# Two exponentials moved ahead of four copies on ScalarE, and the running maxima read from SBUF: one change to a convolution and attention kernel

## The chip, the cores and the metric

The kernel runs on one core of a Trainium2 chip. The core has a matrix engine (TensorE, PE in the profile; PEld is its loading of weights), a vector engine (VectorE, DVE), a scalar engine for activation functions (ScalarE, ACT), GpSimd (POOL) and SyncE (SP), on whose queue this kernel's transfers are issued. Each executes its own instructions in the order of the program and waits on semaphores for the others. Tiles lie in SBUF (128 partitions); results of matrix products lie in PSUM, which has 8 banks of 128x512 fp32 words here, and are taken out by DVE or ACT. The metric is the time of one execution on the device, in microseconds (us); less is better. Unless something else is said, durations come from one profiled execution.

## What is computed

The input x has the shape (8, 512, 32, 32) in fp32. Two layers run, each on a group-normalised x and each added back to it.

```python
# layer 0; cbs(x, w) = silu(batch_norm(conv(x, w)))
t = cbs(gn(x), cv1_w)                       # 1x1, 512 -> 512
ys = [t[:, :256], t[:, 256:]]
for i in range(2):
    yi = ys[-1]
    z = cbs(yi, m_cv1_w[i])                 # 3x3, 256 -> 256
    qkv = conv(z, qkv_w[i])                 # 1x1, 256 -> 768, four heads of 64
    logits = einsum('bhdi,bhdj->bhij', q, k + r) * 64 ** -0.5    # 1024 x 1024
    a = softmax(logits, axis=-1)
    z = einsum('bhij,bhdj->bhdi', a, v)
    ys.append(yi + cbs(z, m_cv2_w[i]))      # 1x1, 256 -> 256
x = x + cbs(concatenate(ys, axis=1), cv2_w) # 1x1, 1024 -> 512
# layer 1: a 1x1 convolution, 512 -> 512, its weights masked and permuted by a gate
x = x + conv(gn(x), w_eff)
```

## The kernel before

**Units.** The attention is cut into 64 units: an image, one of its two bottlenecks, a pair of heads (hp) and a half (512) of the 1024 queries. Sixteen slots of four units follow each other, with the images taken in pairs. A unit holds its logits transposed: the 1024 keys are 8 tiles (KT = 8) of 128 partitions, and one tile is a pair of 128x512 halves, one for each head, stored as one 128x1024 tile `st` in SBUF (the pool `stp` has 10 of them).

**Steps.** A unit is worked off in four steps of two tiles (`for t in range(0, KT, 2)`, lines 1055 to 1082). While unit u is exponentiated and multiplied by its values, the logits of the next unit (`nxt`) are made. In a step:

- `u.soften(t)`, `u.soften(t + 1)` (line 545, DVE): adds to `st` the negated maximum of each query, which lies spread over all partitions in PSUM (`mb`).
- `exponent` (line 549, ACT): the exponential of a 128x1024 tile in place; POOL then adds it in four pieces to the running sum (line 556).
- `lag.values` (line 563, PE): the products of the exponentials with the values, into the one bank `po`. They lag by one step: step 0 works off the last two tiles of the unit before, step 2 tiles 0 and 1 of this unit.
- At step 0 also `before.finish()` (line 577 on PE, the sum's reduction over partitions; line 580 on ACT, the copy of these denominators to `rb`) and `before.divide` (DVE: two reciprocals of 128x256, line 584, and two multiplications of `po` into `q`, line 586). The second of these is the last reader of `po`, so the next unit's first values wait for it.
- `nxt.logits(t)`, `nxt.logits(t + 1)`: eight products on PE in the profile (line 511) fill four PSUM banks; ACT copies each half to `st` (line 518), and from the second tile of a unit on DVE takes the maximum of what was so far (`mx`; of tile 0's `st` at first) and the logits in PSUM, half by half (line 523).
- Last `advance(...)`: convolutions are put onto PE until their share of the slot is reached. A hand-made clock with due times decides which: the 1x1 convolutions cv1, cv2, m_cv2 and that of layer 1 (all line 175 on PE, outputs `cv`, `m` and `l`), the 3x3 convolution by Winograd products (line 313, output `m`), and the projection to q, k and v (lines 175 and 405). ACT takes most of them out of PSUM with a SiLU (line 130, outputs `y`, `m2s`, `cv2s`, `z`) and normalises x (line 165, `x`); DVE adds residuals (line 430 `ybuf` and `res`, line 457 `xr`, line 487 `x2r`).

After the last step, `top` (line 531 on PE, 532 on DVE) transposes and reduces `mx` to one maximum for each query, and `spread` (line 540, `mb`) spreads it.

**What sets the order.** ACT's copies and exponentials are tied in the order in which the program issues them (`act_turn`); DVE's additions of line 545, maxima and a few others by `in_turn`, PE's attention products by `pe_turn`. All other instructions are placed by a scheduler between these, each on its engine, before the kernel runs; their order is fixed then.

**Buffers.** Of PSUM's 8 banks, `mb` holds two, `po` one; the other five (`bank`, line 68) go round among the logits, the denominators, the transposed maxima and all convolutions. A product into such a bank waits until the last reader of what was in it is done. An exponential and a SiLU need different tables on ACT; a switch is an instruction of its own (ACT_TABLE_LOAD), which the profile puts down to the line of the activation after it (130 or 549).

Of the kernel before, what the change touches and what calls it, by code (L numbers as in the profile page):

```python
# [17 lines left out]
ALU = mybir.AluOpType  # L18
# [21 lines left out]
def conv_preact_kernel(ctx: ExitStack, tc: tile.TileContext, x, cv1, cv2, mcv1, qkv, mcv2, bn, rw, rh, conv, s_in, t_in, out):  # L40
    nc = tc.nc
# [23 lines left out]
    def pair(p, tag, name):  # L65
        return p.tile([P, 2, HALF], F32, tag=tag, name=name)

    def bank(name):
        return ps_f.tile([P, HALF], F32, tag="bank", name=name)
# [4 lines left out]
    def flat(t):  # L74
        return t.rearrange("p a b -> p (a b)")
# [106 lines left out]
    def in_turn(instruction):  # L182

        if turn:
            tc.add_manual_dep(instruction.ins, turn.pop().ins.name, IN_ORDER, reason="order of VectorE")
        turn.append(instruction)

    def act_turn(instruction):

        if act_last:  # L190
            tc.add_manual_dep(instruction.ins, act_last.pop().ins.name, IN_ORDER, reason="order of ScalarE")
        act_last.append(instruction)
# [3 lines left out]
    def pe_turn(instruction):  # L196

        if pe_last:
            tc.add_manual_dep(instruction.ins, pe_last.pop().ins.name, IN_ORDER, reason="order of TensorE")
        pe_last.append(instruction)  # L200
# [293 lines left out]
    class Unit:  # L494
# [8 lines left out]
        def logits(self, t):  # L503

            if t == 0:
                self.begin()
            lg = [bank(f"lg_{self.name}_{t}_{h}") for h in range(2)]
            for h in range(2):
                r = slice(HD * h, HD * h + HD)
                pe_turn(  # L510
                    nc.tensor.matmul(  # L511
                        lg[h], self.k[r, ts(t, P)], self.q[r, self.hp, ts(self.half, HALF)], start=True, stop=True
                    )
                )
            st = pair(stp, "st", f"st_{self.name}_{t}")
            self.st.append(st)
            for h in range(2):
                act_turn(nc.scalar.copy(st[:, h], lg[h]))  # L518
            if t == 1:
                self.mx = pair(one, "mx", f"mx_{self.name}")  # L520
            for h in range(2 if t else 0):
                so_far = self.st[0] if t == 1 else self.mx
                in_turn(nc.vector.tensor_tensor(self.mx[:, h], so_far[:, h], lg[h], ALU.max))  # L523

        def top(self):

# [382 lines left out]
    def slot_filler(s):  # L909

        prev = slots[s - 1] if s else (None, 0)
        nxt = slots[s + 1] if s + 1 < len(slots) else (None, 0)
        todo, needed = [], 0.0

        def add(us, g):
            nonlocal needed
            todo.append((us, g))
            needed += us

        im, i = nxt  # L920
        add(8.0, bg.take(8.0))
        if im and i == 1:
            add(7.0, im.conv_m2(0))
            add(0.0, call(im.transform, 1, 3.0, 1.0))
            add(9.0, bg.take(9.0))
        products = im.conv3(i) if im else iter(())
        if prev[1] == 1:
            if im:
                add(21.3, (us for _, us in zip(range(16), products)))
            add(7.0, prev[0].conv_m2(1))  # L930
            add(0.0, call(lambda: finishing(prev[0])))
        if im:
            add(10.7 if prev[1] == 1 else 32.0, products)
            add(7.0, bg.take(7.0))
        if im:
            add(21.0, im.project(i))
        if s + 2 < len(slots) and slots[s + 2][1] == 0:
            add(0.0, call(slots[s + 2][0].load_y))
            add(0.0, call(slots[s + 2][0].transform, 0, 8.0, 1.3))
        rest = SHARE - needed if im else 70.0  # L940
        if rest > 0:
            todo.append((rest, bg.take(rest, wait=True)))
        total = sum(c for c, _ in todo)
        return needed, total, todo
# [77 lines left out]
    for s in range(len(slots)):  # L1022
        needed, total, todo = slot_filler(s)
        state = {"done": 0.0}

        def filler():
            for us, g in todo:
                start = state["done"]
                for cost in g:
                    clock.tick(cost)  # L1030
                    state["done"] += cost
                    yield

                state["done"] = max(state["done"], start + us)

        fill = filler()

        def advance(share):
            goal = max(share * total, min(1.0, share / 0.74) * needed + 0.1)
            while state["done"] < goal:  # L1040
                if next(fill, "end") == "end":
                    break

        steps = 4 * (KT + 2)
        for j in range(4):
            u = units[4 * s + j]
            nxt = units[4 * s + j + 1] if 4 * s + j + 1 < len(units) else None
            base = j * (KT + 2)

            advance((base + 0.7) / steps)  # L1050
            u.top()
            clock.tick(0.9)
            advance((base + 1.4) / steps)
            u.spread()
            clock.tick(0.9)
            advance((base + 2) / steps)
            for t in range(0, KT, 2):
                if before and t == 0:
                    before.finish()
                    clock.tick(0.9)  # L1060
                u.soften(t)
                u.soften(t + 1)
                if t:
                    u.exponent(t)

                lag = u if t else before
                if lag:
                    lag.values((t - 2) % KT)
                    lag.values((t - 1) % KT)
                    clock.tick(2.0)  # L1070
                if before and t == 0:
                    before.divide(0)
                    before.divide(1)
                if nxt:
                    nxt.logits(t)
                    nxt.logits(t + 1)
                    clock.tick(2.0)

                if not t:
                    u.exponent(t)  # L1080
                u.exponent(t + 1)
                advance((base + 4 + t) / steps)
            before = u
        for _ in fill:
            pass
# [62 lines left out]
```

## Time and profile before

| | us |
|---|---|
| median of three runs | 3184.22 (3184.0 to 3186.14) |
| the profiled execution | 3188.51 |
| its span, from the first to the last instruction | 3186.8 |
| mean granted TensorE clock | 0.993 |
| one step, typically | about 9.2 |
| eight products of a step's logits (line 511) | 1.99 |
| eight products of a step's values (line 563) | 1.94 |
| copy of 128x512 from PSUM, ACT (line 518) | 0.596 |
| exponential of 128x1024, ACT (line 549) | 1.068 |
| table load, ACT | 1.283 |
| SiLU of 128x512, ACT (line 130) | 0.777 |
| copy of denominators, ACT (line 580) | 0.583 |
| maximum of 128x512, DVE (line 523) | 0.681 |
| addition of 128x1024, DVE (line 545) | 1.213 |
| reciprocal of 128x256, DVE (line 584) | 1.723 |

A line of the profile's groups names the line of the kernel, the engine, the operation, its output and inputs (names without buffer numbers), the shape and the count; behind the first bar stand the busy time in us and the mean of one in ns, behind the second the engine's idle time just before these instructions and what ended most of it. A timeline's line gives the start and the length in us of a run of like instructions, and in brackets the idle time before it and what ended that. The end of a matrix product is modelled, so products that follow each other overlap by up to 0.1 us in such lines.

A second view of the same execution, in 40 slices, shows that PE is busy throughout:

```profile
PE   7999999999999999999999999999999999999999
DVE  5446576667666676667666676667766676666742
ACT  3255765854655555544656455554656455555631
```

Each digit is the busy share of a slice in tenths; the first slices are the preparation of weights and the first two images, and the units run from about 215 us to 3060 us.

### The profile page before, as it was taken

The page shows a single profiled execution, that of the slowest core. Times are in us where ns is not written, and L with a number is a line of the kernel's source. Part 1 is how long each engine was busy: PE and PEld are TensorE (multiplying, and loading weights), DVE is VectorE, ACT ScalarE, POOL GpSimd, SP SyncE. Part 2 cuts the span into 40 slices and gives each one's busy share as a digit, 9 for nine tenths or more (in the row PEclk, how much of TensorE's full clock was granted, in tenths as well). Part 3 has the DMA queues.
Part 4 walks back from the last instruction along what each step waited for, and adds up shares of the span by engine and source line. Part 5 has one row for each costly group of instructions (what it writes and reads, how often), then busy time and mean ns, then how long its engine had stood idle before and what let it go on. Part 6 is the DMA issues. An engine that isn't in the chain of part 4 may idle for free.

```text
span 3186.8 us, 34171 instructions
## 1 busy us (share of the span) xinstructions
PE 3085.9 (97%) x11668; PEld 1522.9 (48%) x11668; DVE 2050.6 (64%) x2718; ACT 1717.3 (54%) x2347; POOL 1395.3 (44%) x1867
## 2 busy tenths in 40 slices
PE   7999999999999999999999999999999999999999
PEld 3645444454445454454445454454445454453333
DVE  5446576667666676667666676667766676666742
ACT  3255765854655555544656455554656455555631
POOL 2114444446444454445444454355434454455420
PEclk9999999999999999999999999999999999999999
DMA  8851442421233232424233332424233332413366
GB/s 294 287 187 63 154 161 83 149 79 65 88 109 129 93 119 70 148 86 137 89 109 129 119 114 75 139 83 142 90 113 132 110 122 71 145 63 129 110 212 216
DMA packets 142014, 399.35 MB, mean 125 GB/s; under 512 B 13072, under 2 KB 14352, under 8 KB 141840
## 3 DMA queue, kind: packets, MB, share of 16 engines
q1 hardware_dynamic: 141120, 396.94, 36.4%
q8 instruction: 92, 1.51, 0.2%
q14 instruction: 82, 0.67, 0.1%
q10 hardware_dynamic: 720, 0.23, 0.0%
HBM read 317.42 MB, written 79.69 MB: 125 GB/s over the span
## 4 chain that ended last, share of the span: by engine, by line
PE 70%; DVE 7%; ACT 5%; issue 3%; DMA 2%; POOL 1%; ACTq 0%; DVEq 0%; SPq 0%; POOLq 0%
PE m L313 14%; PE cv L175 12%; PE lg L511 11%; PE po L563 11%; PE qk L175 6%; PE l L175 6%; PE v L405 3%; PE m L175 2%; DVE st L545 2%; PE mb L540 2%; ACT st L518 2%; PE mt L531 2%; PE den L577 2%; DVE mx L523 1%; ACT st L549 1%
## 5 line engine op out<-in xcount | busy, mean ns | idle before, releaser
L556 POOL TENSOR_TENSOR sum<-sum,st 128x256 f32<-128x256 f32 x1536 | 1126.1, 767 | 570.1 <-ACT st L549 565.0
L523 DVE TENSOR_TENSOR mx<-mx,lg 128x512 f32<-128x512 f32 x768 | 477.8, 681 | 412.2 <-ACT st L518 412.2
L549 ACT ACTIVATE st<-st 128x1024 f32<-128x1024 f32 x512 | 539.1, 1068 | 340.2 <-DVE st L545 338.8
L518 ACT COPY st<-lg 128x512 f32<-128x512 f32 x1024 | 524.4, 596 | 351.7 <-PE lg L511 306.6
L545 DVE TENSOR_TENSOR st<-st,mb 128x1024 f32<-128x1024 f32 x512 | 603.7, 1213 | 63.6 <-PE mb L540 63.6
L313 PE MATMUL m<-plane,w_m 128*128 128x256 f32 x2304 | 537.4, 388 | 21.8 <-DVE x2r L487 9.0
L556 POOL TENSOR_TENSOR sum<-st,st 128x256 f32<-128x256 f32 x256 | 188.0, 766 | 789.4 <-ACT st L549 789.3
L563 PE MATMUL po<-st,v 128*64 128x512 f32 x2048 | 500.3, 608 | 21.7 <-ACT st L549 14.7
L511 PE MATMUL lg<-q,k 64*128 64x512 f32 x2048 | 513.7, 619 | 1.6 <-ACT y L130 1.5
L313 PEld LDWEIGHTS m<-plane,w_m 128*128 128x128 f32 x2304 | 433.0, 192 | 149.0 <-issue 44.1
L175 PE MATMUL cv<-y,w_cv 128*128 128x512 f32 x1024 | 465.4, 599 | 10.8 <-DVE mx L523 6.2
L511 PEld LDWEIGHTS lg<-q,k 64*128 64x128 f32 x2048 | 178.6, 187 | 330.1 <-issue 266.4
L175 PEld LDWEIGHTS cv<-y,w_cv 128*128 128x128 f32 x1024 | 185.7, 190 | 251.7 <-issue 227.8
L563 PEld LDWEIGHTS po<-st,v 128*64 128x64 f32 x2048 | 128.9, 137 | 327.5 <-issue 228.9
L175 PE MATMUL l<-x,w_l 128*128 128x512 f32 x512 | 235.8, 603 | 10.3 <-DVE mx L523 10.0
L175 PE MATMUL cv<-x,w_cv 128*128 128x512 f32 x512 | 233.4, 603 | 8.5 <-ACT x L165 2.4
L175 PE MATMUL qk<-z,w_qkv 128*128 128x512 f32 x512 | 234.0, 600 | 1.7 <-DVE mx L523 1.7
L584 DVE RECIPROCAL rb<-rb 128x256 f32<-128x256 f32 x128 | 215.4, 1723 | 30.6 <-ACT rb L580 30.5
L532 DVE TENSOR_REDUCE nm<-mt 128x4 f32<-128x512 f32 x128 | 82.4, 685 | 158.6 <-PE mt L531 158.5
L580 ACT COPY rb<-den 128x512 f32<-128x512 f32 x64 | 37.3, 583 | 226.9 <-PE den L577 226.9
L175 PEld LDWEIGHTS l<-x,w_l 128*128 128x128 f32 x512 | 92.7, 190 | 132.3 <-issue 107.2
L175 PEld LDWEIGHTS cv<-x,w_cv 128*128 128x128 f32 x512 | 94.3, 192 | 126.4 <-issue 107.3
(145 smaller groups left out, 2404.3 us busy)
## 6 DMA issues: line engine op xcount, KB each, us to landing
w_m<-w_m SPq DMA_DIRECT2D x96, 768.0 KB, 4.8
w_cv<-in_cv SPq DMA_DIRECT2D x90, 512.0 KB, 3.5
y<-y SPq DMA_DIRECT2D x64, 512.0 KB, 4.4
x<-in_x SPq DMA_DIRECT2D x56, 512.0 KB, 5.4
y<-y SPq DMA_DIRECT2D x64, 256.0 KB, 3.5
k<-r SPq DMA_DIRECT2D x32, 512.0 KB, 3.6
res<-y SPq DMA_DIRECT2D x32, 512.0 KB, 4.0
xr<-in_x SPq DMA_DIRECT2D x32, 512.0 KB, 4.0
```

The lines of the kernel that those rows point to most:

```text
L175: nc.tensor.matmul(ps, w, moving, start=(n == 0), stop=(n == len(terms) - 1))
L313: nc.tensor.matmul(ps[:, ts(co, 256)].rearrange("p (t x) -> p t x", x=F), w[:, co, c, dx], u[:, 9 * c : 9 * c + 8, dx : dx + F], start=(j ...
L405: nc.tensor.matmul(ps[:, ts(j, P)], z[:, c, ts(4 * j4 + j, P)], w[:, c, 512 + P * hp : 512 + P * hp + P], start=(c == 0), stop=(c == IT - 1),)
L511: nc.tensor.matmul(lg[h], self.k[r, ts(t, P)], self.q[r, self.hp, ts(self.half, HALF)], start=True, stop=True)
L518: act_turn(nc.scalar.copy(st[:, h], lg[h]))
L523: in_turn(nc.vector.tensor_tensor(self.mx[:, h], so_far[:, h], lg[h], ALU.max))
L532: nc.vector.tensor_reduce(self.nm[:, h], mt, AX.X, ALU.max, negate=True)
L545: in_turn(nc.vector.tensor_tensor(st, st, flat(self.mb), ALU.add))
L549: act_turn(nc.scalar.activation(st, st, AF.Exp))
L556: nc.gpsimd.tensor_tensor(flat(self.acc)[:, part], flat(so_far)[:, part], st[:, part], ALU.add)
L563: nc.tensor.matmul(self.po[HD * h : HD * h + HD], self.v[:, t, ts(h, HD)], self.st[t][:, h], start=(t == 0), stop=(t == KT - 1),)
L584: nc.vector.reciprocal(self.rb[:, r], self.rb[:, r])
```

## The change

Two edits. In `logits`, the maximum of a tile becomes one operation on the whole 128x1024 pair, which reads the copy `st` in SBUF where it read the two halves in PSUM. In the step's loop, the exponentials of tiles 0 and 1 are issued ahead of the last values of the unit before, of its division and of the next unit's logits; so far both stood behind these. In the other steps the order stays: the first tile's exponential ahead, the second's behind the logits.

```diff
@@ -518,9 +518,10 @@
                 act_turn(nc.scalar.copy(st[:, h], lg[h]))
             if t == 1:
                 self.mx = pair(one, "mx", f"mx_{self.name}")
-            for h in range(2 if t else 0):
+            if t:
+
                 so_far = self.st[0] if t == 1 else self.mx
-                in_turn(nc.vector.tensor_tensor(self.mx[:, h], so_far[:, h], lg[h], ALU.max))
+                in_turn(nc.vector.tensor_tensor(flat(self.mx), flat(so_far), flat(st), ALU.max))
 
         def top(self):
 
@@ -1060,8 +1061,10 @@
                     clock.tick(0.9)
                 u.soften(t)
                 u.soften(t + 1)
-                if t:
-                    u.exponent(t)
+                u.exponent(t)
+                if not t:
+
+                    u.exponent(1)
 
                 lag = u if t else before
                 if lag:
@@ -1076,9 +1079,8 @@
                     nxt.logits(t + 1)
                     clock.tick(2.0)
 
-                if not t:
-                    u.exponent(t)
-                u.exponent(t + 1)
+                if t:
+                    u.exponent(t + 1)
                 advance((base + 4 + t) / steps)
             before = u
         for _ in fill:
```

`flat` views a pair of halves as one row of 1024. `exponent(1)` also issues tile 1's four sums on POOL, which move with it.

## The prediction

> **What bounds the kernel now.** I read the page first, then the list of what TensorE (PE) waits for between 220 and 3030 us (the 64 units), then timelines around single waits.
>
> ```profile
> span 3186.8 us, 34171 instructions
> PE 3085.9 (97%) x11668; PEld 1522.9 (48%) x11668; DVE 2050.6 (64%) x2718; ACT 1717.3 (54%) x2347; POOL 1395.3 (44%) x1867
> ...
> L523 DVE TENSOR_TENSOR mx<-mx,lg 128x512 f32<-128x512 f32 x768 | 477.8, 681 | 412.2 <-ACT st L518 412.2
> L549 ACT ACTIVATE st<-st 128x1024 f32<-128x1024 f32 x512 | 539.1, 1068 | 340.2 <-DVE st L545 338.8
> L518 ACT COPY st<-lg 128x512 f32<-128x512 f32 x1024 | 524.4, 596 | 351.7 <-PE lg L511 306.6
> L545 DVE TENSOR_TENSOR st<-st,mb 128x1024 f32<-128x1024 f32 x512 | 603.7, 1213 | 63.6 <-PE mb L540 63.6
> ```
>
> PE is busy for all but 3186.8 − 3085.9 = 100.9 us. VectorE (DVE) and ScalarE (ACT) idle for over a third of the span, so removing work from DVE shortens nothing by itself. The change can win only PE's waits, and PE loses only where a new wait reaches it. Whose waits these are:
>
> ```profile
> PE po L563 <- ACT st L549: 14.7, 12, 3.7
> PE l L175 <- DVE mx L523: 10.0, 5, 2.6
> PE m L313 <- DVE x2r L487: 9.0, 3, 3.5
> PE cv L175 <- DVE mx L523: 8.2, 7, 2.0
> ...
> PE po L563 <- DVE mx L523: 6.9, 8, 2.3
> ...
> PE m L313 <- DVE mx L523: 2.1, 5, 1.5
> ...
> PE qk L175 <- DVE mx L523: 1.7, 1, 1.7
> ```
>
> Columns: us in total, times, longest. Convolutions (l, cv, m, qk) wait for a maximum because it is the last reader of the PSUM bank they need: 10.0 + 8.2 + 2.1 + 1.7 = 22.0 us. The value products (po) wait for an exponential or, by their label, a maximum: 14.7 + 6.9 = 21.6 us. So 43.6 us are the most that the change can address. One bank wait, and two waits of po:
>
> ```profile
> 1626.27 2.02 ACT L518 COPY st<-lg 128x512 f32<-128x512 f32 x4
> ...
> 1626.86 2.48 DVE L523 TENSOR_TENSOR mx<-mx,lg 128x512 f32<-128x512 f32 x4 [0.46 <-ACT st L518]
> ...
> 1627.61 3.70 PE L175 MATMUL cv<-y,w_cv 128*128 128x512 f32 x8 [1.47 <-DVE mx L523]
> ```
>
> ```profile
> 1441.07 2.02 PE L563 MATMUL po<-st,v 128*64 128x512 f32 x8 [1.23 <-DVE mx L523]
> ...
> 2917.66 3.68 PE L563 MATMUL po<-st,v 128*64 128x512 f32 x8 [3.72 <-ACT st L549]
> ```
>
> In the first, the copy of the first half ends at 1626.87, its maximum at 1627.54, and PE starts 0.07 later: the bank came free 0.67 us after its copy. In the second, the value products of a unit's first tile stand still until its exponential is done, which stands behind the next unit's four copies on ACT.
>
> **What the skill says.** "VectorE: DVE Perf Modes" (section on the TRN2 errata) gives an fp32 tensor_tensor as (N+151)/0.96 ns: 691 for N=512 and 1224 for N=1024. The trace agrees within 2%: 681 for the maxima (whose one source is in PSUM), 1213 for L545's add of 128x1024. "PSUM — Partial Sum Buffer" (PSUM bank collisions) says that two engines may not be in the same bank and quadrant at once, reads included; hence the maximum cannot overlap the copy of the same bank, and the trace shows maxima idle 412.2 us until a copy ends. "ScalarE: Activation LUTs" (What ACT_TABLE_LOAD costs) gives about 1283 ns for a load at every switch between sets of functions, plus a drain of 1380; the trace has the load at 1283 and the next exponential 0.01 after it, so I use 1.28 without the drain. "TensorE: Matmul & The Clock Gate" (HAM clock gate) says that an idle PE falls to half clock; here the 3.72 us wait above is followed by po taking 3.68 instead of 1.94.
>
> **The maxima.** Out: 896 maxima (768 + 128 of the first form) of 0.68. In: 448 of 128x1024, both operands in SBUF, as L545's shape: 1.22. Busy time falls by 896×0.68 − 448×1.22 = 63 us, but back to back they start 0.60 and 1.13 us apart, so a backlogged step gains only 4×0.60 − 2×1.13 = 0.14. Where DVE keeps pace with the copies (0.48 apart), the first maximum now waits for two copies and the step ends 0.48 − 0.14 = 0.34 later. Neither is on PE's path unless DVE ends late. What reaches PE is the bank, free at the copy's end. Eight waits like the one shown (at 343.5, 440.7, 527.6, 908.2, 1457.9, 1627.6, 2179.0, 2348.8) lose 0.7 each, but at 343.5 the maximum was held up by group-norm statistics and all 2.1 go: 7×0.7 + 2.1 = 7.0. Four smaller (near 667, 1191, 1910, 2628) give 0.22 each: 0.9. Together 7.9. The last layer's waits near 1308, 2027 and 2745, with a second some 14 us later (0.66 and 2.3 to 2.6 each, 9.2 in all), I count as nothing: DVE there runs a chain (residual load of 7.35 us, its additions, L545, exponential, copies, maxima) that ends in m's wait for x2r, the 9.0 us above, which takes back what is gained ahead of it.
>
> **The first exponentials.** Tiles 0 and 1 go ahead of the four copies. Nothing is added but their order. In the unit from 1433.10 us (first mb transpose; times below are from such a start) the first exponential ended at 7.91 and po started at 7.96. The second L545 ends at 3.50 and the copy of the denominators (L580) at 2.70, so the two exponentials can run from 2.7 to 4.7, before the first copy at 4.91. Then po's bank decides: its last reader, the second division (L586), ends at 7.38. Gain 0.53, not 1.23. By the same subtraction: units 7, 27, 43, 59: 4×0.53 = 2.1; 28, 44: 0.8; 23, 39, 55: 0.87 each = 2.6 (0.37, and 0.5 because the copies of tile 2 no longer wait for POOL's sum, 45.0 us of ACT's idle time over 23 times); 11, 12, 19: 0.5 + 0.6 + 1.3 = 2.4; 16, 32, 48: 0.6; unit 60: 3.72 becomes 1.7 (division at 7.59, exponential was at 9.56), and 1.5 of its slow matmuls. Sum 2.1 + 0.8 + 2.6 + 2.4 + 0.6 + 3.5 = 12.0.
>
> **What that puts in the way.** ACT executes in the program's order, and that order shows 40 more table loads (262 for 222): exponentials now stand between SiLUs. Forty loads are 51 us of an engine that idles 46%; only those ahead of a copy matter. The worst is unit 3 (start 349.65):
>
> ```profile
> 354.73 0.76 ACT L130 ACTIVATE y<-cv,bn_b,bn_s 128x512 f32<-128x512 f32 x1
> 355.39 0.57 ACT L580 COPY rb<-den 128x512 f32<-128x512 f32 x1
> 356.39 2.05 ACT L518 COPY st<-lg 128x512 f32<-128x512 f32 x4 [0.43 <-PE lg L511]
> 358.46 1.28 ACT L549 ACT_TABLE_LOAD   x1
> 359.75 2.00 ACT L549 ACTIVATE st<-st 128x1024 f32<-128x1024 f32 x2
> ```
>
> After: x, x (to 5.2), load, exponential 0, load, SiLU, denominators, load, exponential 1, copies. From 5.2: 1.28 + 1.07 + 1.28 + 0.78 + 0.57 + 1.28 + 1.07 = 12.5, so the first copy ends near 13.0; it ended at 7.33. The group of cv matmuls that follows needs its bank at 7.69 and waits 12.97 − 7.69 = 5.3. Unit 4 (396.72) has the same order with a late x in it: copy at 16.4 for 11.6, PE waits 4.85 more. After each, slow matmuls: 2 together, by unit 60's case. Ten units have this order; in the other eight (6, 8, 16, 24, 32, 40, 48, 56) copies come some 1.7 later by the same addition, but PE finds their banks free when it asks: 0 (at worst 1.7 each, 13.6). Units 13, 17, 29, 33, 45, 49 put exponential 2 between two loads ahead of the last m2s SiLU, whose bank m's next product wants at 14.74 and gets near 15.3: 6×0.55 = 3.3. Units 20, 36, 52: the later maxima delay a cv2s chain by 0.3: 0.8 (bounds 0 and 3). On POOL the sums start earlier with exponential 1; SP's loads keep their order but for a few swaps, cost 0. Losses 5.3 + 4.85 + 2 + 3.3 + 0.8 = 16.3.
>
> **Sum.** −7.9 − 12.0 + 16.3 = −3.6. On the profiled execution, 3188.51 (span 3186.8 and 1.7 around it), that is 3184.9; on the median shown, 3184.22, it is 3180.6. I say 3180.5.
>
> **Rivals.**
> (1) Small gain as summed, own range 3174 to 3187: 0.42.
> (2) Larger gain. If the last layer's maxima waits go too (9.2) and the banks at units 3 and 4 turn out free, it is 7.9 + 12.0 + 9.2 − 4.1 = 25 us; with only one of the two 13 to 16. I take 19, between these: 3165. For: 43.6 us of waits name these lines. Against: the divisions end at 7.4 to 7.6, and x2r waits for a DMA. 0.27.
> (3) No change, 3184: every earned wait comes back as another's (divisions, x2r). For: PE at 97%. Against: the bank waits have nothing else behind them. 0.09.
> (4) Slower, by one mechanism: table loads and exponentials ahead of the copies hold PSUM banks, at the eight further units too. It decides from the point where a copy ends after PE asks for its bank. Then 3180.6 + 13.6 = 3194. For: five banks only, and units 3 and 4 show it. Against: at several of the eight the copies already stood behind POOL's sum (up to 3.4 us) and end about where they did. 0.22.
>
> 0.2% is 6.4 us, about what can be told from no change. Under 3177.8: nearly all of (2), 0.26, and a good third of (1), 0.16: 0.42. Over 3190.6: three quarters of (4), 0.17, and 0.05 of the others: 0.22. Between: 0.36. The range runs from just under (2)'s 3165 to just under (4)'s 3194: 3163 to 3193.
>
> **What would show it.** Right: no wait of a convolution for a maximum outside the last layer's places; po's first wait in unit 27 at 0.7; 40 more table loads; waits of cv of about 5 us near 357 and 405. Wrong: no such waits, or x2r's 9.0 us gone (then 2), or waits for copies in the eight units (then 4).

## The result: slower by 1.6%

The changed kernel took 3238.68 us in the median (3228.86 to 3240.2), the kernel before 3184.11 (3183.04 to 3186.14): a ratio of 1.016, with a 95% interval from 1.0142 to 1.0178. The prediction was 3180.5 in a range of 3163 to 3193, so both the sign and the range were wrong.

The page of the kernel after, with the rows that answer to those shown of before (the lines of the file have moved by one: 523 is now 524, 545 is 546, 549 is 550, 556 is 557, 563 is 564, 540 is 541):

```profile
span 3237.7 us, 33432 instructions
PE 3106.1 (96%) x11668; PEld 1535.4 (47%) x11668; DVE 2118.6 (65%) x2270; ACT 1770.7 (55%) x2387; POOL 1612.7 (50%) x1867
...
L557 POOL TENSOR_TENSOR sum<-sum,st 128x256 f32<-128x256 f32 x1536 | 1333.5, 902 | 751.1 <-ACT st L550 750.5
...
L524 DVE TENSOR_TENSOR mx<-mx,st 128x1024 f32<-128x1024 f32 x384 | 535.8, 1395 | 444.9 <-ACT st L518 423.8
...
L546 DVE TENSOR_TENSOR st<-st,mb 128x1024 f32<-128x1024 f32 x512 | 603.9, 1213 | 63.6 <-PE mb L541 60.6
```

Of the 51 us by which the span grew, PE's idle time holds 31: 3237.7 − 3106.1 = 131.6 us where it was 100.9. The other 20 are products that took longer: the same 11668 of them are busy for 3106.1 us instead of 3085.9, at a mean granted clock of 0.988 for 0.993. On its losing side the prediction had put slower products at 2 us.

DVE has 448 instructions fewer and is busy for longer, 2118.6 us for 2050.6. POOL does exactly what it did before, 1867 instructions, and is busy for 1612.7 us instead of 1395.3. The two rows that carry this are the maxima, 1.395 us where I had put 1.22, and POOL's sums, 0.902 for 0.767. The addition of L546, from which the 1.22 was taken, still takes 1.213. Besides the operation itself it differs in one thing: its second operand, `mb`, lies in PSUM, while both operands of the new maximum lie in SBUF.

What PE waits for between 220 and 3080 us in the kernel after (us in total, times, longest):

```profile
PE m L313 <- DVE x2r L487: 14.5, 3, 4.8
PE m L313 <- ACT cv2s L130: 13.6, 3, 4.5
PE l L175 <- ACT st L518: 10.0, 5, 2.4
PE m L313 <- ACT st L518: 9.1, 7, 4.1
PE po L564 <- DVE q L587: 8.9, 10, 1.8
PE po L564 <- ACT st L550: 6.5, 4, 2.7
PE mb L541 <- DVE nm L533: 5.3, 4, 4.3
```

The intended part happened. No convolution waits for a maximum any more (22.0 us before), and po's waits for exponentials fell from 14.7 to 6.5. Others took their place: x2r from 9.0 to 14.5, cv2s from 8.2 to 13.6, mb for nm from 0.7 to 5.3, and the same banks' waits for ACT's copies, 10.0 for l and 9.1 for m.

### The profile page after: what moved, and what is told of

Same layout as the page of the kernel before. It is cut to its first block, busy times and chain, and to the rows that moved or that the text cites. A ratio compares the mean times of both kernels' runs of the same rounds, so it can differ in the third digit from the quotient of the medians.

```text
span 3237.7 us, 33432 instructions
## 1 busy us (share of the span) xinstructions
PE 3106.1 (96%) x11668; PEld 1535.4 (47%) x11668; DVE 2118.6 (65%) x2270; ACT 1770.7 (55%) x2387; POOL 1612.7 (50%) x1867
## 3 DMA queue, kind: packets, MB, share of 16 engines
q8 instruction: 93, 1.52, 0.2%
## 4 chain that ended last, share of the span: by engine, by line
PE 64%; DVE 11%; ACT 4%; issue 3%; DMA 2%; POOL 2%; SPq 0%; DVEq 0%; ACTq 0%; POOLq 0%
PE cv L175 14%; PE m L313 11%; PE lg L511 9%; PE po L564 9%; PE qk L175 6%; PE l L175 6%; PE v L405 3%; DVE st L546 3%; DVE mx L524 2%; POOL sum L557 2%; PE mt L532 2%; PE mb L541 1%; PE den L578 1%; DVE rb L585 1%; ACT st L518 1%
## 5 line engine op out<-in xcount | busy, mean ns | idle before, releaser
L557 POOL TENSOR_TENSOR sum<-sum,st 128x256 f32<-128x256 f32 x1536 | 1333.5, 902 | 751.1 <-ACT st L550 750.5
L524 DVE TENSOR_TENSOR mx<-mx,st 128x1024 f32<-128x1024 f32 x384 | 535.8, 1395 | 444.9 <-ACT st L518 423.8
L546 DVE TENSOR_TENSOR st<-st,mb 128x1024 f32<-128x1024 f32 x512 | 603.9, 1213 | 63.6 <-PE mb L541 60.6
L313 PE MATMUL m<-plane,w_m 128*128 128x256 f32 x2304 | 547.7, 393 | 43.8 <-DVE x2r L487 14.5
```

The costliest lines, as they stand in the source:

```text
L313: nc.tensor.matmul(ps[:, ts(co, 256)].rearrange("p (t x) -> p t x", x=F), w[:, co, c, dx], u[:, 9 * c : 9 * c + 8, dx : dx + F], start=(j ...
L524: in_turn(nc.vector.tensor_tensor(flat(self.mx), flat(so_far), flat(st), ALU.max))
L546: in_turn(nc.vector.tensor_tensor(st, st, flat(self.mb), ALU.add))
L557: nc.gpsimd.tensor_tensor(flat(self.acc)[:, part], flat(so_far)[:, part], st[:, part], ALU.add)
```

## The experiments

Two theories stood against each other. T1: two operands in SBUF put DVE and POOL in each other's way, and DVE's lateness costs most of the time. T2: the exponentials and table loads ahead of copies and SiLUs on ACT, rival (4) of the prediction, cost most of it. All ratios are to runs of the kernel before on the same chip; on these later occasions it took 3188 to 3190 us in the median. The ratios are not quotients of the medians, but lie within 0.0012 of them.

| kernel | median us | ratio to before | 95% interval |
|---|---|---|---|
| maxima alone | 3220.49 | 1.0102 | 1.0083 to 1.0120 |
| exponentials alone | 3201.25 | 1.0038 | 1.0024 to 1.0051 |
| maxima alone, without most sums | 3153.05 | 0.9881 | 0.9863 to 0.9900 |
| before, without most sums | 3150.13 | 0.9875 | 0.9859 to 0.9891 |
| maxima of halves, both from the copies | 3258.63 | 1.0215 | 1.0200 to 1.0231 |
| maxima of halves, one from the copies | 3203.20 | 1.0041 | 1.0027 to 1.0055 |
| exponentials ahead from unit 5 on | 3182.69 | 0.9977 | 0.9967 to 0.9987 |
| exponentials unsplit | 3203.65 | 1.0037 | 1.0024 to 1.0050 |
| both of these | 3187.23 | 0.9997 | 0.9989 to 1.0004 |
| exponentials ahead in 18 chosen units | 3173.85 | 0.9955 | 0.9938 to 0.9972 |

### The change taken apart

Maxima alone, the exponentials as before:

```diff
-            for h in range(2 if t else 0):
+            if t:
                 so_far = self.st[0] if t == 1 else self.mx
-                in_turn(nc.vector.tensor_tensor(self.mx[:, h], so_far[:, h], lg[h], ALU.max))
+                in_turn(nc.vector.tensor_tensor(flat(self.mx), flat(so_far), flat(st), ALU.max))
```

> The maxima alone: one 128x1024 maximum from the copies in SBUF, exponentials as before. In the changed kernel a maximum took 1.40 us on average, not the 1.22 of the prediction: 1.22 where no POOL sum ran beside it, 1.52 where one ran for most of it, and POOL's sums took 0.90 for 0.77. Theory T1 (the two operands in SBUF hinder POOL and are hindered by it; late maxima are most of the loss): 3210 to 3240 us, with maxima near 1.4 us and the waits of m for cv2s and x2r long (13 and 14 us in all). Theory T2 (the exponentials and table loads ahead of the copies and SiLUs on ScalarE are most of the loss): 3175 to 3195, the bank waits gone, and cv2s and x2r waits only a little longer than before.

Exponentials alone, the maxima as before:

```diff
-                if t:
-                    u.exponent(t)
+                u.exponent(t)
+                if not t:
+                    u.exponent(1)
...
-                if not t:
-                    u.exponent(t)
-                u.exponent(t + 1)
+                if t:
+                    u.exponent(t + 1)
```

> The exponentials alone: tiles 0 and 1 ahead, maxima from PSUM as before. T1: 3172 to 3190, since the maxima cost 0.68 as before and ScalarE's order costs only the 12 us of units 3 and 4, against 12 us gained. T2: 3205 to 3235, with units 0, 3 and 4 alone longer by 20 us or more, as in the changed kernel (5.6, 13.3 and 5.8 us).

Both parts lose. The maxima cost 1.0%, about 32 us (31 by the medians), as T1 said. The exponentials cost 0.4%, about 12 us, which lies between the two expectations, though units 0, 3 and 4 lose the 20 us of T2 (table below). Their sum, 1.4%, agrees with the 1.6% of both within the intervals. One detail of T1 failed: with the maxima alone m waits 13.7 us for cv2s, as expected, but only 9.5 for x2r, for which 14 had been expected and 9.0 stood before. The 14.5 of the changed kernel stands in neither part alone (9.5 and 10.6).

The way from a late maximum to PE can be followed in unit 52, at the same place of both kernels. First the timeline of the kernel before, with the lines of DVE, ACT and PE that form the chain:

```profile
2571.14 2.48 DVE L523 TENSOR_TENSOR mx<-mx,lg 128x512 f32<-128x512 f32 x4 [3.49 <-ACT st L518]
2573.54 1.82 DVE L430 TENSOR_TENSOR ybuf<-res,m2s 128x512 f32<-128x512 f32 x2
...
2580.66 1.06 ACT L549 ACTIVATE st<-st 128x1024 f32<-128x1024 f32 x1 [7.14 <-DVE st L545]
...
2583.86 2.43 PE L313 MATMUL m<-plane,w_m 128*128 128x256 f32 x10 [2.71 <-ACT cv2s L130]
```

Then the timeline of the kernel with the maxima alone, with POOL's line beside them:

```profile
2597.69 8.67 POOL L557 TENSOR_TENSOR sum<-sum,st 128x256 f32<-128x256 f32 x7
...
2597.85 1.64 DVE L524 TENSOR_TENSOR mx<-mx,st 128x1024 f32<-128x1024 f32 x1 [3.97 <-ACT st L518]
...
2599.95 1.22 DVE L524 TENSOR_TENSOR mx<-mx,st 128x1024 f32<-128x1024 f32 x1 [0.46 <-ACT st L550]
...
2601.09 2.34 DVE L430 TENSOR_TENSOR ybuf<-res,m2s 128x512 f32<-128x512 f32 x2
...
2608.74 1.06 ACT L550 ACTIVATE st<-st 128x1024 f32<-128x1024 f32 x1 [8.99 <-DVE st L546]
...
2611.94 4.63 PE L313 MATMUL m<-plane,w_m 128*128 128x256 f32 x10 [4.56 <-ACT cv2s L130]
```

Before, the four maxima took 2.48 us. Now the first of the two starts 0.48 later in its unit, because it waits for two copies, and takes 1.64 beside POOL. The second begins after a gap of 0.46, and the pair ends 3.32 after its start. The additions to `ybuf`, which also read two tiles in SBUF, take 2.34 for 1.82: before, the second of them took 1.22 beside a sum and the first 0.68; now each takes 1.21. By then DVE is 1.8 us late, and so are the exponential (idle for 8.99 instead of 7.14 us), the SiLU to cv2s behind it, and PE: it waits 4.56 instead of 2.71, and after this the first ten products of m take 4.63 for 2.43. This is the cv2s chain that the prediction named, and for which it had put 0.3 us. It is not the whole loss: the three units with this chain (20, 36 and 52) are 7.1 us longer with the maxima alone, units 11, 12, 24 and 56 another 14.6, unit 0 6.1. What PE waits for in those others was not traced unit by unit.

### POOL taken away

The same two kernels with POOL's sums of tiles 2 to 7 left out. The edit, made to the maxima alone and to the kernel before:

```diff
-            for j in range(4 if t else 0):
+            for j in range(4 if t == 1 else 0):
...
-                nc.gpsimd.tensor_tensor(flat(self.acc)[:, part], flat(so_far)[:, part], st[:, part], ALU.add)
+                two = [v.rearrange("p (a b) -> p a b", b=P) for v in (flat(self.acc)[:, part], st[:, part])]
+                nc.gpsimd.tensor_tensor(two[0], ones.unsqueeze(1).to_broadcast([P, 2, P]), two[1], ALU.add)
```

> The maxima alone, with POOL's sums of tiles 2 to 7 left out and tile 1's made with ones (the softmax denominators are then others). T1: a maximum takes 1.22 us again, and the time falls clearly below that of the maxima alone with all sums, by 15 us or more, to near the kernel before without these sums. T2: maxima may be 1.22, but the time stays within 6 us of the maxima alone with all sums.

> The kernel before, with the same sums left out. Both theories: 3170 to 3184, since its maxima do not meet POOL; only copies that wait for a sum (45 us of ScalarE's idle time) come earlier. Under T1 the two kernels without sums lie within 6 us of each other; under T2 as well, so this run serves only as the baseline of the one beside it.

Without these sums the maxima alone are 3 us from their baseline (3153.05 against 3150.13, overlapping intervals) instead of 31. The row of the maxima in the kernel that has them alone, without the sums:

```profile
L524 DVE TENSOR_TENSOR mx<-mx,st 128x1024 f32<-128x1024 f32 x384 | 472.4, 1230 | 476.6 <-ACT st L518 457.0 <-DVE mx L524 0.9
```

1.230 us, as the prediction had it: the duration was right for a DVE that has SBUF to itself. The baseline itself fell by 1.25%, far more than expected: the sums delay this kernel beyond what they do to maxima. Its trace shows two ways. The additions of L457, which read two tiles in SBUF, take 0.764 us for 0.886, and ACT's copies, which before waited 45.0 us for sums, no longer wait for any. How much of the 38 us each is worth is not shown.

### Size or operands

In the kernel with the maxima alone a maximum also waits for two copies and is twice as large. To keep these apart, the maxima stay 896 of 128x512, but read the copies:

```diff
-                in_turn(nc.vector.tensor_tensor(self.mx[:, h], so_far[:, h], lg[h], ALU.max))
+                in_turn(nc.vector.tensor_tensor(self.mx[:, h], so_far[:, h], st[:, h], ALU.max))
```

> Exponentials as before; the maxima stay 896 of 128x512, but read the logits from the copies in SBUF, both halves. No maximum waits for two copies. T1 (two SBUF operands against POOL's sums): maxima above 0.72 us on average, sums again above 0.85, and 15 to 35 us over the kernel before. Rival T5 (the maxima alone lose because the one operation waits for both copies): maxima 0.69 or less, sums 0.77, within 6 us of the kernel before or below it, since the banks come free at the copies.

And only the second half, with `st[:, h] if h else lg[h]` in the same place:

> As the one with both halves from the copies, but only the second head's half; the first still reads PSUM. T1: about half its loss, 7 to 18 us over the kernel before, with the two forms of maximum apart by 0.05 us or more. T5: within 6 us of the kernel before.

With both halves from the copies the loss doubles, to 2.15%, some 69 us and about twice the most that T1 had expected; with one it is 0.41%, as T1 had it. T5, the wait for both copies, falls as the main cause: it is absent here and the loss is larger. (In unit 52 it was 0.48 of the 1.8 us.) The groups by form, first of the kernel with both halves from the copies, then of that with one:

```profile
L556 POOL TENSOR_TENSOR sum<-sum,st 128x256 f32<-128x256 f32 x1536 | 1342.7, 909 | 482.0 <-ACT st L549 481.9
L523 DVE TENSOR_TENSOR mx<-mx,st 128x512 f32<-128x512 f32 x768 | 722.7, 997 | 338.0 <-ACT st L518 337.8
```

```profile
L523 DVE TENSOR_TENSOR mx<-mx,st 128x512 f32<-128x512 f32 x384 | 289.9, 755 | 2.2 <-ACT st L518 2.2
L523 DVE TENSOR_TENSOR mx<-mx,lg 128x512 f32<-128x512 f32 x384 | 261.6, 681 | 398.9 <-ACT st L518 398.9
```

In one and the same kernel the form that reads PSUM takes 0.681 and the one that reads SBUF 0.755; with both halves from SBUF it is 0.997. Twice as many instructions meet a sum nearly twice as often: 270 of the 448 merged maxima began while a sum ran, and 517 of the 896 halves. So the merged maximum is the lesser evil of the two: over all maxima it lost (634.5 − 448×1.22) = 88 us of DVE's time when alone, and the halves lost (810.7 − 559.6) = 251.

### The order on ACT

Exponentials ahead only from unit 5 on, by a condition `early = 4 * s + j >= 5` on the moved calls:

> Maxima as before; the exponentials of tiles 0 and 1 go ahead only from unit 5 on. Theory T3 (the exponentials alone lose only where ScalarE puts them ahead of SiLUs and copies whose banks PE asks for, which is in the first five units; elsewhere they gain): the exponentials in all units made units 0 to 4 longer by 23.3 us and all others together shorter by 17, so 17 us under the kernel before (ratio 0.9947, 0.993 to 0.997). Rival T4 (the loss of the first units is a matter of their start and returns at whatever units come first, or the gain is disturbed with it): within 6 us of the kernel before.

Exponentials ahead in all units, with the two additions exchanged at step 0, so that both become ready together:

```diff
-                u.soften(t)
-                u.soften(t + 1)
+                u.soften(t + (t == 0))
+                u.soften(t + (t != 0))
```

> Maxima as before; exponentials ahead in all units, but the additions of tiles 0 and 1 change places on VectorE at step 0, so that both exponentials become ready together and no SiLU is put between them: 234 table loads instead of 262. If the loads and SiLUs between the exponentials made the loss (T3): units 3 and 4 lose half or less of the 7.8 and 9.7 us they lost with the exponentials alone, and the time is 0 to 10 us under the kernel before. If it is the exponentials ahead of the copies as such, whatever stands between: the same as the exponentials alone, 6 to 12 us over the kernel before.

Both edits:

> Both: exponentials ahead from unit 5 on, additions exchanged at step 0 in all units. T3: as the first or a little better, 15 to 22 us under the kernel before (ratio 0.993 to 0.9955). T4: within 6 us of it.

The lengths of some units, from one unit's first mb product to the next one's, as differences from the kernel before (us, one profiled execution each; that of the exponentials alone was 6.5 us under its median, so its units add up to about half of the 12 us):

| unit | both parts of the change | exponentials alone | unsplit | from unit 5 on |
|---|---|---|---|---|
| 0 | +5.6 | +4.2 | +2.1 | +1.2 |
| 3 | +13.3 | +7.8 | +5.1 | +1.0 |
| 4 | +5.8 | +9.7 | +7.2 | +0.4 |
| 11 | +1.4 | −3.0 | −1.6 | −3.0 |
| 15 | −1.7 | −1.7 | −1.7 | −1.7 |
| 19 | +3.2 | +3.2 | +3.4 | +3.2 |
| 60 | −3.9 | −4.3 | −4.3 | −4.3 |

From unit 5 on, the exponentials gain 0.23%: the loss of units 0 to 4 is gone and has not moved to the units that now come first. This is the direction of T3, but 7 us and not 17: the ratio lies outside T3's range and just beyond the 6 us of its rival T4. Unit 0 is a weak witness, since it was 6.1 us longer with the maxima alone too. The unsplit order does not save the first units. It has 234 table loads for 262, and units 3 and 4 still lose 5.1 and 7.2, with the total as slow as that of the exponentials alone. So T3's detail falls: it isn't mainly the loads and SiLUs between the exponentials that hurt. What is left are the two exponentials (and the load ahead of them), standing before copies whose banks PE is about to need; this is what remains, and no run shows it by itself. Both edits together bring nothing, where T3 had 15 to 22 us. Beside exponentials ahead from unit 5 on, then, the exchange of the additions costs some 6 us of its own (0.9997 against 0.9977), so the totals of the unsplit kernels say less than their units.

Unit 3 of the changed kernel shows it on PE's own timeline:

```profile
363.35 1.87 PE L511 MATMUL lg<-q,k 64*128 64x512 f32 x2 [1.95 <-ACT y L130]
365.15 0.59 PE L156 MATMUL gv_a<-gd_a,gmat 128*128 128x4 f32 x2
366.67 7.27 PE L175 MATMUL cv<-x,w_cv 128*128 128x512 f32 x12 [0.93 <-ACT st L518]
```

The unit starts at 353.89, so the cv products start at 12.8; before they started at 7.7. That is the 5.3 us of the prediction to within a few tenths, though it comes in pieces: the logits themselves wait 1.95 for a bank that a SiLU has not yet emptied, then cv for the copy. After it the twelve products take 7.27 for 5.40. What was not foreseen is the end of the unit, where PE waits 4.34 us for nm. On DVE nm, the reduced maxima, stands behind group-norm statistics, which idle three times for a load of x, the last time 1.48 us until 412.33, just ahead of nm at 413.53. With the exponentials alone the same wait is 0.37, so the loads of x did not meet nm there.

### A version that beats both

Exponentials ahead only in the 18 units that were shorter for it with the exponentials alone (`early = 4 * s + j in (7, 11, 15, 16, 23, 24, 31, 32, 36, 39, 40, 47, 48, 55, 56, 59, 60, 62)`), maxima from PSUM:

> Maxima as before; exponentials ahead only in the 18 units in which the kernel with them in all units was shorter than before by its profile. If the gains of units stand alone: about 25 us under the kernel before (ratio 0.990 to 0.995). If they are only paid back from losses of their neighbours: between the kernel before and the one with exponentials ahead from unit 5 on (0.9967 to 1.000).

3173.85 us, 0.45% under the kernel before: faster than both kernels, at 14 us of the 26 that the single units add up to. In its profile the 18 units are 22.0 us shorter and all others together 6.6 longer. So the gains of units do not simply add; why is not shown.

## Why the prediction was wrong, by its own steps

**The maxima: the step that failed.** The prediction wrote "In: 448 of 128x1024, both operands in SBUF, as L545's shape: 1.22", and with this price DVE's lateness came to a loss of 0.8 us, against 7.9 gained from the banks. L545 has the same shape but not the same operands. Beside a sum on POOL for more than half of their length, the changed kernel's maxima took 1.52 us on average and L546's additions 1.21, the same as without one; where no sum ran beside them the maxima took 1.22. The profile of the kernel before already held this in two rows of one shape, the first with both tensors in SBUF, the second with one (`l`) in PSUM:

```profile
L457 DVE TENSOR_TENSOR xr<-xr,cv2s 128x512 f32<-128x512 f32 x64 | 56.7, 886 | 118.7 <-ACT cv2s L130 118.1
L487 DVE TENSOR_TENSOR x2r<-l,x2r 128x512 f32<-128x512 f32 x64 | 43.7, 685 | 42.1 <-PE l L175 32.5 <-DMA x2r<-x 9.5
```

With nothing on POOL beside it the first took 0.69 too; where POOL worked for more than half of its length, 1.05. Alone, the maxima cost about 32 us instead of gaining 7.1; without most of the sums, 3. "SBUF — State Buffer" in the Trainium skill (Who interferes with whom) says it: a DVE instruction with two inputs in SBUF contends with a GpSimd instruction that reads SBUF, one with at most one input there does not. This trace agrees on both sides (1.52 and 1.21). The prediction looked up the price of the operation and not who else uses its operands' memory; POOL's 1314 us of sums (1126.1 + 188.0) stood in the page.

**Who is hurt.** "Neither is on PE's path unless DVE ends late" was right as a sentence, and the condition then came true. The prediction had DVE at 64% and took that for slack. The chain of unit 52 has none: it needs DVE, ACT and PE in turn. The 0.3 us put on it was 1.8, the mechanism right and the size six times too small; the three units with it lost 7.1 where 0.8 was forecast.

**Bank waits.** Right: they are gone. But their 7.9 us can't be seen in any total, since copies and late results of DVE took their place in the list of waits. (The sum was also 0.3 us too high: the four waits put at 0.22 are 0.16 to 0.17 in the trace, and the one of 2.1 is 2.03.)

**The first exponentials.** The gains, measured with the exponentials alone, came in part: unit 60 gained 4.3 where 3.5 was forecast, and unit 11 gained 3.0 where it was 0.5, but all the units named add up to 7.7 of the forecast 12.0. In unit 27 the wait fell from 1.23 to 0.79 us and its releaser became the division, as forecast (0.7), but the unit did not get shorter. Unit 19, put down as a gain of 1.3, lost 3.2. The losses of units 3 and 4 were forecast at 12.2 with the slow products and measured at 17.5. The six units with exponential 2 between two loads lost 3.6 where 3.3 was forecast. Unit 0, 4.2 longer, does not appear in the prediction; nor do gains of units 15, 31, 40, 47 and 56, 11.6 together. As a whole, exponentials alone were forecast at about +3.5 us (16.3 − 12.0, less the 0.8 for maxima) and measured at +12.

**The rivals.** (4) had the right sign and one of the two causes, the smaller: the exponentials do hold banks. Its place was wrong, since the eight further units of that order did not lose for it with the exponentials alone, and it lacked the larger cause. No rival had DVE's new operands as a cost.

What stays open: how the 32 us divide between DVE's lateness and POOL's, as both are slowed by the same meeting. The traces point to DVE. Copies wait for sums less than before (25.4 us with the maxima alone, for 45.0), so POOL's delay does not reach them. And over the kernels with one half, merged maxima and both halves from the copies, the losses of 13, 32 and 69 us follow DVE's added busy time (43, 94 and 260) and not POOL's (106, 272 and 220). No run separates the two. Open too is why the exponentials' gains by unit add up to more than the kernel from unit 5 on gained.

## What to carry to other kernels

Price a moved operand by a row with the same memories, not only the same shape: for a DVE operation with two tensors, ask whether one of them comes from PSUM, and which sums of POOL run beside it. A read of PSUM that looks like a nuisance, since it holds a bank for 0.7 us longer, can be what keeps two engines apart. And an engine's share of busy time isn't slack where PE waits at the end of a chain that goes through it.

## What the runs showed of the hardware

- The same 128x1024 maximum took 1.22 us with no sum on POOL beside it and 1.52 with a sum beside it for more than half of its length; the sums that lay for over nine tenths of their length beside a maximum took 1.65 us, for 0.73 in the kernel before. Each waits for the other's whole instruction: in the changed kernel 260 of the 263 sums that began during a maximum ended 0.58 to 0.61 us after its end, and 214 of the 226 maxima that began during a sum ended 1.08 to 1.13 after its end. In the kernel before, where the maxima read PSUM, the first of these is spread from 0.05 to 0.73.
- Smaller pieces make it worse: the 768 maxima of 128x512 that took both operands from SBUF and read `mx` took 1.00 us for 0.68, and all 896 lost nearly three times what the merged ones did.
- Slow products followed the longer waits of PE here: twelve of cv took 7.27 us instead of 5.40 after the waits in unit 3, and ten of m took 4.63 after one of 4.56. After one of 2.71, in the kernel before, the same ten took 2.43.
